# A two-layer megakernel: the plan of layer 0 with eight single PSUM banks

## Chip, cores and metric

One core of a Trainium2 chip runs the whole kernel in one launch. The metric is device time in microseconds. TensorE (PE) multiplies, VectorE (DVE) and ScalarE (ACT) read its results out of PSUM, GpSimd (POOL) works on SBUF alone, and SyncE (SP) issues the loads. PSUM has eight banks of 128 x 512 float32; TensorE writes a product into a bank, and another engine must read it before the bank can be written again.

## What is computed

Two layers over 2 sequences of 1024 tokens with 256 channels. The change touches only layer 0:

```python
# layer 0, attention: 16 query heads of 16 channels, 8 key/value heads
xn = layernorm(x)
q, k, v = xn @ W_Q.T, xn @ W_K.T, xn @ W_V.T
q, k = rope(q), rope(k)
scores = einsum('bsdkg,btdk->bkgst', q, k) / sqrt(256)
ctx = softmax(scores) @ v
s = ctx @ W_O.T
# layer 0, feed-forward: weights are a 16-entry table looked up by index
gate, up = xn @ lut[gate_idx].T, xn @ lut[up_idx].T
y = (silu(gate) * up) @ lut[down_idx].T
x = x + s * silu(y)
```

So the feed-forward does not need the attention, only its weights and xn; the two meet at the end. Layer 1 is a gated recurrence over 128-token chunks and a mixture of eight experts with a shared one; its code is the same in both kernels.

## The kernel before

**Blocks.** Attention runs in sixteen blocks (g, h): g counts batch and group of four heads, h the half of 512 queries. In a block the four heads lie in four groups of 32 rows of the TensorE array (`SLOT`), so matmuls of different heads, which have different rows, can run side by side. A block has four kinds of work:

- *maxima* (`largest`, L570 to L600): for each of 4 query chunks, 2 halves of the keys and 2 pairs of heads, TensorE makes the products mx of two heads (L582, two matmuls a head), and VectorE takes the largest of each row from both in one reduction (L598). 16 products and 16 reductions a block.
- *shift* (L602): from these maxima VectorE makes the negative shift, TensorE transposes it (mTp, L635), ScalarE copies it (mT, L642).
- *scores* (`weigh`, L644 to L668): for each of 8 key chunks and 2 pairs of heads, TensorE makes the transposed scores sc of two heads (L654, three matmuls a head: two of q and k, one that adds the shift), and ScalarE takes the exponential of each (L666). 16 products and 32 exponentials a block.
- *gather* (`gather`, L670): for each key chunk TensorE adds the four heads' exponentials times v into cx (L679, eight instructions in the trace). After the eighth, ScalarE copies cx, TensorE transposes it (ctp, L701) and VectorE divides (L708, L709).

**Other steps of layer 0.** `chunks` normalises, projects and rotates the tokens (qkv L439, transposes L411, L524); `project_out` makes s (so, L742); `decode` (L759) turns the indices into weights in nine pieces: for each of 16 table entries a comparison ("pick", L768) on GpSimd or, for the pieces of `DVE_PIECES`, on VectorE, and an addition on GpSimd (L785); `feed` (L795) is the feed-forward in four blocks of 512 tokens (gate and up L813, down L861), which needs all nine pieces. Its first two blocks compute silu by Tanh, which ScalarE has loaded together with Exp, the last two by Silu, which needs another table.

**The plan.** None of these steps is placed by hand. Each is an entry of the class `Plan`: an engine, a cost in us, what it reads and writes, and a due number `when`. `write_order` (L190) goes through a model of time: of all steps whose inputs are done and whose buffers are free it takes the one that can start first, and among those the one with the smallest `when`; it emits the step and moves the engine's clock on by the cost. The order in which steps are emitted is the order in which each engine will run them. A row product (maxima or scores) looks for a second one with other rows (`_mates`, L158); if there is one, the two are emitted as a team, round by round, so that four matmuls stand next to each other. `TURN` and `SOLO` are surcharges on `when` for a change of kind of work and for a row product without a mate.

**Buffers.** Slots are taken from pools when a step is placed (`_take`, L168) and come free after their last reader. The eight PSUM banks stand in three pools: "bank" with three single ones (scores and all transposes and projections), "pair" with two of two neighbouring banks each (maxima), "sum" with one (cx). The plan does not write the waits: the layer below it adds a semaphore wait wherever an instruction touches what another engine's earlier instruction touched.

Layer 1 follows in another order, made by the tile layer's own scheduler.

Of the kernel before, what the change touches and what calls it, by code (L numbers as in the profile page):

```python
# [11 lines left out]
F32 = mybir.dt.float32  # L12
# [8 lines left out]
P = 128  # L21
# [15 lines left out]
NQT = 4  # L37
# [58 lines left out]
class Plan:  # L96
# [71 lines left out]
    def _take(self, step):  # L168
        for t in step.slots:
            if t.slot is None:  # L170
                p = self.pools[t.pool]
                p["free"].sort()
                _, t.slot = p["free"].pop(0)
                p["held"][t.part] = p["held"].get(t.part, 0) + 1
                t.ap = p["pool"].tile(
                    list(t.shape), t.dtype, tag=f"{t.pool}{t.slot}", name=t.name, bufs=1
                )

    def _drop(self, step, end):
        for t in step.slots:  # L180
            t.left -= 1
            t.end = max(end, getattr(t, "end", 0.0))
            if t.left == 0:
                p = self.pools[t.pool]
                p["free"].append((t.end + 0.08, t.slot))
                p["held"][t.part] -= 1

    LAG = {"PE": 0.2, "ACT": 0.12, "DVE": 0.1, "POOL": 0.12, "SP": 0.0}

    def write_order(self, log=None):  # L190
# [4 lines left out]
        while left:  # L195
            best = None
            for e in self.ENGINES:
                if best and clock[e] > best[0]:
                    continue
                for s in ready[e]:  # L200
# [21 lines left out]
            if s.engine == "PE" and s.mode != mode:  # L222
                start += 0.1
            self._take(s)
            ready[s.engine].remove(s)
            if s.passes:
                for x in self._mates(s, ready["PE"], start + 0.05)[:1]:
                    team.append(x)
                    self._take(x)
                    ready["PE"].remove(x)  # L230
                rounds = max(len(x.passes) for x in team)
                for r in range(rounds):
                    for x in team:
                        if r < len(x.passes):
                            for _, emit in x.passes[r]:
                                emit()
                clock["PE"] = start + rounds * self.ROW
                ends = [start + len(x.passes) * self.ROW for x in team]
            else:
# [7 lines left out]
            for x, end in zip(team, ends):  # L247
                left -= 1
                self._drop(x, end)
                for y in x.next:  # L250
# [8 lines left out]
def first_layer(nc, tc, xs, xnT, s_sb, ident, epst, x_v, wqkv_d, rope_d, lut_d, idx_d, wo_d, sel_d):  # L259

    psum = bass.MemoryType.PSUM
    with ExitStack() as st:
        att = st.enter_context(tc.tile_pool(name="att", bufs=1))
        slots = st.enter_context(tc.tile_pool(name="slots", bufs=1))
        ps1 = st.enter_context(tc.tile_pool(name="ps1", bufs=1, space=psum))
        st.enter_context(tc.manual_schedule())
        plan = Plan(
            tc,
            {
                "bank": (ps1, [P, 512], 3, {}),  # L270
                "pair": (ps1, [P, 2, 512], 2, {}),
                "sum": (ps1, [P, 512], 1, {}),
                "two": (slots, [P, 512], 26, {"e": 13, "f": 16}),
                "q": (slots, [P, 512], 10, {}),
# [9 lines left out]

        def bank(name):
            return Slot("bank", [P, 512], name)

# [65 lines left out]
        STAT = 4  # L353
        qhls, kTs, qTs, tops, mTs, cxs, sums, ctxs, es = {}, {}, {}, {}, {}, {}, {}, {}, {}

# [213 lines left out]

        def largest(g, h, c, half, pair, when):  # L570

# [3 lines left out]
            top = tops[g, h]  # L575
            ps = Slot("pair", [P, 2, 512], f"mx{g}_{h}_{c}_{half}_{pair}")
            qT, kT = qTs[g, h], kTs[b, T // 2]

            def product(k, x):
                i = 2 * pair + k  # L580
                at = slice(SLOT * i, SLOT * (i + 1))
                nc.tensor.matmul(  # L582
                    ps.ap[:, k, :],
                    qT.ap[at, ts(c, P)],
# [9 lines left out]
            need = (qT, (kT, 2 * half), (kT, 2 * half + 1)) if half else (qT, (kT, 0), (kT, 1))  # L594
            add(PE, 0.43, None, need, (ps,), when, "rows", passes)

            def reduce():
                nc.vector.tensor_reduce(top.ap[:, c, 2 * pair : 2 * pair + 2, half], ps.ap, AX.X, ALU.max)  # L598

            add(DVE, 1.22, reduce, (ps,), ((top, c, half, pair),), when)  # L600

# [41 lines left out]

        def weigh(g, h, c, pair, when):  # L644
            b, T = divmod(g, NQT)
            qT, kT, mT = qTs[g, h], kTs[b, T // 2], mTs[g, h]
            pss = [bank(f"sc{g}_{h}_{c}_{2 * pair + k}") for k in range(2)]

# [9 lines left out]
            ]  # L658
            add(PE, 0.65, None, (qT, (kT, c // 2), mT, "sel"), pss, when, "rows", passes)
            for k in range(2):  # L660
                i = 2 * pair + k
                e = two(f"e{g}_{h}_{c}_{i}", part="e")
                es[g, h, c, i] = e

                def soft(k=k, e=e):
                    nc.scalar.activation(e.ap, pss[k].ap, AF.Exp, scale=1.0 / math.sqrt(E))  # L666

                add(ACT, 0.5, soft, (pss[k],), (e,), when + URGENT)  # L668

        def gather(g, h, c, when):  # L670
            b, T = divmod(g, NQT)
            if c == 0:
                cxs[g, h] = Slot("sum", [P, 512], f"cx{g}_{h}")
            cx = cxs[g, h]
# [84 lines left out]
        def decode(piece, when):  # L759
            at = slice(piece * LSTEP, (piece + 1) * LSTEP)  # L760
            codes = two(f"idx{piece}", I32)
            idx = lambda: codes.ap[:, 0:LSTEP]
            add(SP, 3.2, lambda: nc.sync.dma_start(idx(), idx_d[:, at]), (), (codes,), when - 4)
            for j in range(LUT):
                pick = two(f"pick{piece}_{j}") if j else None

# [11 lines left out]
                if piece in DVE_PIECES:  # L778
                    add(DVE, 0.63, choose, (codes, "lut"), (pick or ("w", piece),), w)
                else:  # L780
                    add(POOL, 1.2, choose, (codes, "lut"), (pick or ("w", piece),), w)
                if j:
# [127 lines left out]

        HALF = 8
        chunks(0, lambda c: -60 + 3 * c, True)
        order = [(g, h) for g in range(B * NQT) for h in range(2)]

        def maxima(k):
            g, h = order[k]
            w = HALF * (k - 1) - 4
            turn_q(g, h, w - 2 if k else -51)
            n = 0
            for half in range(2):  # L920
                for c in range(BC):
                    for pair in range(2):
                        largest(g, h, c, half, pair, w + n / 2 if k else -48 + n / 2 + 8 * half)
                        n += 1
            shift(g, h, w + HALF)

        def sums_of(k):
            g, h = order[k]
            w = HALF * k
            for c in range(CPB):  # L930
                for pair in (1, 0):
                    weigh(g, h, c, pair, w + c + (0.5 if pair == 0 else 0.0))
            for c in range(CPB):
                gather(g, h, c, w + c + 2)

        for piece in range(WLUT // LSTEP):
            decode(piece, DECODE_AT[piece])
        for k in range(len(order)):
            maxima(k)
            if k == 1:  # L940
                chunks(1, lambda c: 30 + 2.5 * c, False)
            sums_of(k)
            g, h = order[k]
            if g == NQT - 1:
                for c in range(h * BC, h * BC + BC, 2):
                    project_out(0, c, HALF * k + 14 + c)
            if g == 2 * NQT - 1:
                for c in range(h * BC, h * BC + BC, 2):
                    project_out(1, c, HALF * k + 14 + c)
        for n in range(NBLK):  # L950
# [571 lines left out]
```

## Time and profile before

| what | value |
|---|---|
| median of two runs | 1560.97 us (1558.97 to 1562.96) |
| profiled execution | 1572.11 us, of which the span from first to last instruction is 1570.3 |
| TensorE busy | 1384.5 us, 88% |
| VectorE, ScalarE, GpSimd busy | 743.7, 554.5, 478.0 us |
| mean granted TensorE clock | 0.925 |
| reductions of the maxima, L598 | 256, 304.4 us, 1219 ns each |
| exponentials, L666 | 512, 278.7 us, 595 ns each |
| gathers' matmuls, L679 | 1024, 145.6 us |
| comparisons of the decode on VectorE | 64, 792 ns each |
| table loads of ScalarE before L666, L830 and L875 | 33, 1283 ns each |

The page cuts the span into 40 slices of 39 us and gives each engine's busy share of a slice in tenths. A group's line gives the source line, engine, operation, tile, count, busy time, the mean of one, then the idle time of the engine just before these instructions and what ended it. In a timeline each row is a start, a duration and an instruction, with idle time before it in brackets. Matmuls are pipelined and each is recorded with its latency, so a busy TensorE is not one at its peak. The first matmul of layer 1 starts at 781.68 us.

### The profile page before, as it was taken

The numbers are of one execution on the slowest core, as the hardware profiler recorded it, in microseconds if no ns is written. First come the engines' busy times: TensorE is split into PE (matmuls) and PEld (weight loads), VectorE is DVE, ScalarE is ACT, GpSimd is POOL, SyncE is SP. The second block draws the span as 40 slices with busy tenths as digits, with TensorE's granted clock in tenths as the row PEclk, the third lists the DMA queues.
The fourth block names the chain that finished last, engine by engine and source line by source line (L and its number), as shares of the span: only waits on it lengthen the run. The fifth ranks groups of instructions, "written<-read, shape, count | busy, mean of one in ns | idle before, by whom it ended". The sixth has DMA issues, their size and how long they took to land. (4 is left out here: it accounts for less than half of the span.)

```text
span 1570.3 us, 18022 instructions
## 1 busy us (share of the span) xinstructions
PE 1384.5 (88%) x7272; PEld 730.6 (47%) x7272; DVE 743.7 (47%) x1055; ACT 554.5 (35%) x958; POOL 478.0 (30%) x401
## 2 busy tenths in 40 slices
PE   5899998999999998999686787877777999999998
PEld 2444443444444443434364354544555354453636
DVE  6878887786556444410254265533556312212120
ACT  5256555565544456666412311123211111101010
POOL 7999999896000000000201122210322000010101
PEclk9679998999999999999968889889899999999999
DMA  4000000000000000000220000000000100000000
GB/s 136 1 1 2 1 1 1 1 1 1 1 1 1 1 1 1 1 1 1 75 89 0 0 1 1 0 0 0 1 1 1 47 7 7 0 14 0 14 1 14
DMA packets 8019, 16.80 MB, mean 11 GB/s; under 512 B 1144, under 2 KB 6904, under 8 KB 7424
## 3 DMA queue, kind: packets, MB, share of 16 engines
q1 hardware_dynamic: 7760, 15.58, 2.8%
q8 instruction: 57, 0.93, 0.2%
q14 instruction: 26, 0.21, 0.0%
q10 hardware_dynamic: 144, 0.07, 0.0%
q0 software_dynamic: 32, 0.00, 0.0%
HBM read 13.55 MB, written 2.10 MB: 10 GB/s over the span
## 5 line engine op out<-in xcount | busy, mean ns | idle before, releaser
L598 DVE TENSOR_REDUCE top<-mx 128x2 f32<-128x1024 f32 x256 | 304.4, 1219 | 115.9 <-PE mx L582 98.7
L666 ACT ACTIVATE e<-sc 128x512 f32<-128x512 f32 x512 | 278.7, 595 | 201.4 <-PE sc L654 177.1
L654 PE MATMUL sc<-qT,kT 32*128 32x512 f32 x1024 | 223.7, 464 | 38.1 <-ACT e L666 36.4
L582 PE MATMUL mx<-kT,qT 32*128 32x512 f32 x1024 | 191.4, 461 | 4.9 <-DVE top L598 4.7
L654 PEld LDWEIGHTS sc<-qT,kT 32*128 32x128 f32 x1024 | 95.2, 191 | 209.2 <-issue 108.3
L1250 POOL TENSOR_TENSOR k<-d,kT 128x896 f32<-128x896 f32 x32 | 67.3, 2105 | 342.2 <-ACT d L1246 342.2
L785 POOL TENSOR_TENSOR wlut<-wlut,pick 128x480 f32<-128x480 f32 x135 | 164.6, 1226 | 8.4
L768 POOL TENSOR_SCALAR pick<-idx,lut 128x480 f32<-128x480 int32 x75 | 143.9, 1918 | 11.0 <-PE cx L679 5.3
L679 PE MATMUL cx<-e,v 128*32 128x512 f32 x1024 | 145.6, 629 | 0.8 <-ACT e L666 0.7
L654 PE MATMUL sc<-mT,sel 32*128 32x512 f32 x512 | 126.8, 406 | 0.0
L1400 POOL TENSOR_TENSOR g<-s_sb,g 128x256 f32<-128x256 f32 x16 | 11.6, 722 | 335.7 <-ACT g L1399 335.7
L1238 PE MATMUL dec<-cst,z 128*128 128x512 f32 x128 | 74.8, 704 | 41.9 <-DVE z L1215 31.5
L582 PEld LDWEIGHTS mx<-kT,qT 32*128 32x128 f32 x1024 | 91.6, 200 | 42.5 <-DVE top L598 18.7
L1367 PE MATMUL gu<-xnT,wg 128*128 128x512 f32 (+1 forms) x224 | 110.2, 614 | 1.1 <-issue 1.1
L1375 ACT ACTIVATE sg<-gu 128x512 f32<-128x512 f32 (+1 forms) x56 | 33.4, 597 | 213.5 <-PE gu L1367 213.5
L1367 PE MATMUL gu<-xnT,wu 128*128 128x512 f32 (+1 forms) x224 | 105.6, 593 | 0.0
L1385 DVE TENSOR_TENSOR sg<-sg,share 128x512 f32<-128x512 f32 x44 | 30.2, 687 | 144.5 <-PE share L1378 142.2
L1391 PE MATMUL d<-wd,h 128*128 128x256 f32 x448 | 97.4, 379 | 0.0
L1258 DVE TENSOR_TENSOR d<-d,rT 128x1024 f32<-128x1024 f32 x32 | 52.7, 1647 | 87.0 <-POOL end L1257 86.7
L1284 PE MATMUL lev<-d,k 64*128 64x128 f32 x896 | 76.8, 334 | 17.6 <-DVE d L1258 16.0
L1391 PEld LDWEIGHTS d<-wd,h 128*128 128x128 f32 x448 | 85.1, 190 | 13.5 <-issue 2.0
L1246 ACT ACTIVATE d<-dec 128x1024 f32<-128x1024 f32 x32 | 32.7, 1023 | 165.9 <-PE dec L1238 165.9
(181 smaller groups left out, 1740.8 us busy)
## 6 DMA issues: line engine op xcount, KB each, us to landing
idx<-in_idx SPq DMA_DIRECT2D x9, 240.0 KB, 4.8
out_x<-o SPq DMA_DIRECT2D x16, 128.0 KB, 1.7
wd<-in_wd SPq DMA_DIRECT2D x1, 1792.0 KB, 7.4
wg<-in_wg SPq DMA_DIRECT2D x1, 1760.0 KB
wu<-in_wu SPq DMA_DIRECT2D x1, 1760.0 KB, 12.9
xs<-in_x SPq DMA_DIRECT2D x3, 512.0 KB, 8.0
w<-in_w SPq DMA_DIRECT2D x1, 1536.0 KB, 8.4
cst<-in_cst SPq DMA_DIRECT2D x1, 576.0 KB, 5.4
```

What stands on the lines that cost most here:

```text
L582: nc.tensor.matmul(ps.ap[:, k, :], qT.ap[at, ts(c, P)], kT.ap[at, x, ts(half, 512)], start=(x == 0), stop=(x == 1),)
L598: nc.vector.tensor_reduce(top.ap[:, c, 2 * pair : 2 * pair + 2, half], ps.ap, AX.X, ALU.max)
L654: nc.tensor.matmul(pss[k].ap, lhsT, rhs, start=(x == 0), stop=(x == 2))
L666: nc.scalar.activation(e.ap, pss[k].ap, AF.Exp, scale=1.0 / math.sqrt(E))
L679: nc.tensor.matmul(cx.ap[SLOT * i : SLOT * (i + 1), :], vps[b][:, c, 4 * (T // 2) + i, :], ee[i].ap, start=(c == 0), stop=(c == CPB - 1),)
L768: eng.tensor_scalar(pick.ap[:, 0:LSTEP] if j else wlut[:, at], idx(), float(j), lut[:, j : j + 1], ALU.is_equal, ALU.mult,)
L785: nc.gpsimd.tensor_tensor(wlut[:, at], wlut[:, at], pick.ap[:, 0:LSTEP], ALU.add)
L1238: nc.tensor.matmul(ps[:, h, :], spl[:, k4, ts(m, P)], levels[:, ts(h, 512)], start=True, stop=True,)
L1250: nc.gpsimd.tensor_tensor(k, d[:, 0:NLEV, :], kT1[:, m : m + 1, tok].to_broadcast([P, NLEV, P]), ALU.mult,)
L1284: nc.tensor.matmul(psv[:, par, l2, m, :], lhsT, rhs, start=True, stop=True)
L1367: nc.tensor.matmul(ps[:sz, which, :], w[:, kc, lo : lo + sz], xnT[:, kc, ts(n, 512)], start=(kc == 0), stop=(kc == KC - 1),)
L1391: nc.tensor.matmul(po[:, 0:E], hT[:sz, f, ts(k, P)], wd1[:sz, f, :], start=(f == 0), stop=(f == NF1 - 1),)
```

## The change

Five things, all in layer 0 and its plan:

1. **PSUM.** The pools "bank", "pair" and "sum" become one pool of eight single banks, all views of one tile `banks` of 128 x 8 x 512. At most one is cx, four are maxima, four scores, three anything else ("aux"). A pair of maxima takes any two free banks, lower number first, and its reduction reads both through one access pattern with a step.
2. **Pairing.** `Plan` charges a lone row product in all cases, lets a product wait up to 0.2 us of plan time for its mate, and uses other costs and lags.
3. **Order.** Maxima run a fixed 24 products ahead of the scores, one maxima product due with each score product, with complementary pairs of heads. Batch 1's projections get other due numbers. Exponentials lose their surcharge of 500.
4. **Decode.** Pieces 6, 7 and 8 instead of 5 to 8 go to VectorE; all decode steps get due numbers from 1000 on, the index loads too, so that they come after anything else that could start.
5. **SBUF slots.** The 26 slots of the pool "two" are shared out otherwise: up to 12 for general use instead of 16, 3 for picks and 2 for indices.

In the built order of the changed kernel each engine runs the same work as before apart from the decode piece and 29 table loads less; matmuls of layer 0 are the same in number.

```diff
-DVE_PIECES = (5, 6, 7, 8)
+DVE_PIECES = (6, 7, 8)
-DECODE_AT = tuple(8 * k + (20 if k in DVE_PIECES else 0) for k in range(9))
+DECODE_AT = tuple(1000 + 8 * k for k in range(9))
+GATHER = 2
-    ROW = 0.214
+    ROW = 0.226
+    WAIT = 0.2
-        if engine in ("ACT", "DVE") and any(isinstance(v, Slot) and v.pool == "bank" for v in reads):
+        if engine in ("ACT", "DVE") and any(isinstance(v, Slot) and v.part == "aux" for v in reads):
             when -= URGENT
...
+        new = [t for t in step.slots if t.slot is None]
+        for name in {t.pool for t in new}:
+            p = self.pools[name]
+            p["free"].sort()
+            mine = [t for t in new if t.pool == name]
+            got = sorted(k for _, k in p["free"][: len(mine)])
+            del p["free"][: len(mine)]
+            for t, t.slot in zip(mine, got):
                 p["held"][t.part] = p["held"].get(t.part, 0) + 1
+                if name == "bank":
+                    t.ap = p["pool"][:, t.slot, :]
...
-    LAG = {"PE": 0.2, "ACT": 0.12, "DVE": 0.1, "POOL": 0.12, "SP": 0.0}
+    LAG = {"PE": 0.22, "ACT": 0.17, "DVE": 0.15, "POOL": 0.15, "SP": 0.0}
...
-                        if s.passes and at <= clock[e] and not self._mates(s, ready[e], at):
+                        if s.passes and not self._mates(s, ready[e], at + self.WAIT):
                             late += self.SOLO
...
-                for x in self._mates(s, ready["PE"], start + 0.05)[:1]:
+                for x in self._mates(s, ready["PE"], start + self.WAIT)[:1]:
+                    start = max(start, x.ready, self._room(x))
...
+        banks = ps1.tile([P, 8, 512], F32, name="banks")
-                "bank": (ps1, [P, 512], 3, {}),
-                "pair": (ps1, [P, 2, 512], 2, {}),
-                "sum": (ps1, [P, 512], 1, {}),
-                "two": (slots, [P, 512], 26, {"e": 13, "f": 16}),
+                "bank": (banks, [P, 512], 8, {"sum": 1, "mx": 4, "sc": 4, "aux": 3}),
+                "two": (slots, [P, 512], 26, {"e": 13, "f": 12, "d": 3, "i": 2}),
...
-            ps = Slot("pair", [P, 2, 512], f"mx{g}_{h}_{c}_{half}_{pair}")
+            pss = [bank(f"mx{g}_{h}_{c}_{half}_{2 * pair + k}", "mx") for k in range(2)]
...
             def reduce():
-                nc.vector.tensor_reduce(top.ap[:, c, 2 * pair : 2 * pair + 2, half], ps.ap, AX.X, ALU.max)
-            add(DVE, 1.22, reduce, (ps,), ((top, c, half, pair),), when)
+                lo, hi = pss[0].slot, pss[1].slot
+                i = 2 * pair
+                nc.vector.tensor_reduce(
+                    top.ap[:, c, i : i + 2, half], banks[:, lo : hi + 1 : hi - lo, :], AX.X, ALU.max
+                )
...
+        for i in range(LEAD):
+            w = -48 + i / 2 + (8 if i >= 8 else 0)
+            products(w, maximum(i, w))
+            if i == 15:
+                shift(*order[0], w)
+        for s in range(16 * len(order)):
+            k, j = divmod(s, 16)
+            g, h = order[k]
+            w = s / 2
+            c, pair = j // 2, 1 - j % 2
+            if s == 100:
+                chunks(1, lambda c: 54 + 2 * c, False)
+            products(w, weigh(g, h, c, pair))
+            i = s + LEAD
+            if i < 16 * len(order):
+                products(w, maximum(i, w))
+            if i % 16 == 15 and i < 16 * len(order):
+                shift(*order[i // 16], w)
+            if pair == 0:
+                gather(g, h, c, w + GATHER)
```

`products` adds one TensorE step for the parts it is given, here always one, and then its readers; `maximum` returns the i-th maxima product.

More of the change, by code (lines that the diff above doesn't have):

```diff
@@ L168, in _take @@
     def _take(self, step):
[L169 to L173, printed above, removed]
-                p["held"][t.part] = p["held"].get(t.part, 0) + 1
-                t.ap = p["pool"].tile(
-                    list(t.shape), t.dtype, tag=f"{t.pool}{t.slot}", name=t.name, bufs=1
-                )
+        new = [t for t in step.slots if t.slot is None]
[6 more added lines that the diff above has]
+            for t, t.slot in zip(mine, got):
+                p["held"][t.part] = p["held"].get(t.part, 0) + 1
+                if name == "bank":
+                    t.ap = p["pool"][:, t.slot, :]
+                else:
+                    t.ap = p["pool"].tile(
+                        list(t.shape), t.dtype, tag=f"{name}{t.slot}", name=t.name, bufs=1
+                    )
     def _drop(self, step, end):
@@ L184, in _drop @@
                 p = self.pools[t.pool]
-                p["free"].append((t.end + 0.08, t.slot))
+                p["free"].append((t.end, t.slot))
                 p["held"][t.part] -= 1
-    LAG = {"PE": 0.2, "ACT": 0.12, "DVE": 0.1, "POOL": 0.12, "SP": 0.0}
+    LAG = {"PE": 0.22, "ACT": 0.17, "DVE": 0.15, "POOL": 0.15, "SP": 0.0}
     def write_order(self, log=None):
@@ L223, in write_order @@
                 start += 0.1
+            turn = 0.1 if s.passes and s.mode != mode else 0.0
             self._take(s)
@@ L236, in write_order @@
                                 emit()
-                clock["PE"] = start + rounds * self.ROW
-                ends = [start + len(x.passes) * self.ROW for x in team]
+                clock["PE"] = start + rounds * self.ROW + turn
+                ends = [start + len(x.passes) * self.ROW + turn for x in team]
             else:
@@ L248, in write_order @@
                 left -= 1
-                self._drop(x, end)
+                self._drop(x, end + self.LAG[x.engine])
                 for y in x.next:
@@ L283, in first_layer, with bank @@
         add = plan.add
-        def bank(name):
-            return Slot("bank", [P, 512], name)
+        def bank(name, part="aux"):
+            return Slot("bank", [P, 512], name, F32, part)
         def two(name, dtype=F32, part="f"):
@@ L353, in first_layer @@
         STAT = 4
-        qhls, kTs, qTs, tops, mTs, cxs, sums, ctxs, es = {}, {}, {}, {}, {}, {}, {}, {}, {}
+        qhls, kTs, qTs, tops, mTs, cxs, es, es_all = {}, {}, {}, {}, {}, {}, {}, {}
         def chunks(b, when, first):
@@ L568, in turn_q, with largest @@
             add(ACT, 0.5, lambda: nc.scalar.copy(qT.ap, ps.ap), (ps,), (qT,), when)
-        def largest(g, h, c, half, pair, when):
+        def largest(g, h, c, half, pair):
             b, T = divmod(g, NQT)
@@ L582, in product @@
                 nc.tensor.matmul(
-                    ps.ap[:, k, :],
+                    pss[k].ap,
                     qT.ap[at, ts(c, P)],
@@ L594, in largest @@
             need = (qT, (kT, 2 * half), (kT, 2 * half + 1)) if half else (qT, (kT, 0), (kT, 1))
-            add(PE, 0.43, None, need, (ps,), when, "rows", passes)
             def reduce():
-                nc.vector.tensor_reduce(top.ap[:, c, 2 * pair : 2 * pair + 2, half], ps.ap, AX.X, ALU.max)
-            add(DVE, 1.22, reduce, (ps,), ((top, c, half, pair),), when)
+                lo, hi = pss[0].slot, pss[1].slot
+                i = 2 * pair
+                nc.vector.tensor_reduce(
+                    top.ap[:, c, i : i + 2, half], banks[:, lo : hi + 1 : hi - lo, :], AX.X, ALU.max
+                )
+            return (need, pss, passes), lambda w: add(
+                DVE, 1.14, reduce, pss, ((top, c, half, pair),), w
+            )
         def shift(g, h, when):
@@ L642, in shift, with weigh @@
             add(ACT, 0.5, lambda: nc.scalar.copy(mT.ap, ps.ap), (ps,), (mT,), when)
-        def weigh(g, h, c, pair, when):
+        def weigh(g, h, c, pair):
             b, T = divmod(g, NQT)
             qT, kT, mT = qTs[g, h], kTs[b, T // 2], mTs[g, h]
-            pss = [bank(f"sc{g}_{h}_{c}_{2 * pair + k}") for k in range(2)]
+            pss = [bank(f"sc{g}_{h}_{c}_{2 * pair + k}", "sc") for k in range(2)]
             def product(k, x):
@@ L658, in weigh, with soft, act, rest @@
             ]
-            add(PE, 0.65, None, (qT, (kT, c // 2), mT, "sel"), pss, when, "rows", passes)
             for k in range(2):
[L661 to L665, printed above, removed]
+                es[g, h, c, 2 * pair + k] = two(f"e{g}_{h}_{c}_{2 * pair + k}", part="e")
+            def soft(k):
+                e = es_all[g, h, c, 2 * pair + k]
+                def act():
                     nc.scalar.activation(e.ap, pss[k].ap, AF.Exp, scale=1.0 / math.sqrt(E))
-                add(ACT, 0.5, soft, (pss[k],), (e,), when + URGENT)
+                return e, act
+            es_all.update({(g, h, c, 2 * pair + k): es[g, h, c, 2 * pair + k] for k in range(2)})
+            def rest(w):
+                for k in range(2):
+                    e, act = soft(k)
+                    add(ACT, 0.49, act, (pss[k],), (e,), w)
+            return ((qT, (kT, c // 2), mT, "sel"), pss, passes), rest
+        def products(when, *parts):
+            need, pss, passes = [], [], []
+            for (n, p, q), _ in parts:
+                need += n
+                pss += p
+                for r, x in enumerate(q):
+                    if r == len(passes):
+                        passes.append([])
+                    passes[r] += x
+            add(PE, 0.0, None, need, pss, when, "rows", passes)
+            for _, rest in parts:
+                rest(when)
         def gather(g, h, c, when):
@@ L672, in gather @@
             if c == 0:
-                cxs[g, h] = Slot("sum", [P, 512], f"cx{g}_{h}")
+                cxs[g, h] = bank(f"cx{g}_{h}", "sum")
             cx = cxs[g, h]
@@ L760, in decode @@
             at = slice(piece * LSTEP, (piece + 1) * LSTEP)
-            codes = two(f"idx{piece}", I32)
+            codes = two(f"idx{piece}", I32, "i")
             idx = lambda: codes.ap[:, 0:LSTEP]
-            add(SP, 3.2, lambda: nc.sync.dma_start(idx(), idx_d[:, at]), (), (codes,), when - 4)
+            add(SP, 3.2, lambda: nc.sync.dma_start(idx(), idx_d[:, at]), (), (codes,), when)
             for j in range(LUT):
-                pick = two(f"pick{piece}_{j}") if j else None
+                pick = two(f"pick{piece}_{j}", part="d") if j else None
                 def choose(j=j, pick=pick, eng=nc.vector if piece in DVE_PIECES else nc.gpsimd):
@@ L778, in decode @@
                 if piece in DVE_PIECES:
-                    add(DVE, 0.63, choose, (codes, "lut"), (pick or ("w", piece),), w)
+                    add(DVE, 0.75, choose, (codes, "lut"), (pick or ("w", piece),), w)
                 else:
-                    add(POOL, 1.2, choose, (codes, "lut"), (pick or ("w", piece),), w)
+                    add(POOL, 1.92, choose, (codes, "lut"), (pick or ("w", piece),), w)
                 if j:
@@ L911, in first_layer @@
         HALF = 8
+        LEAD = 24
         chunks(0, lambda c: -60 + 3 * c, True)
         order = [(g, h) for g in range(B * NQT) for h in range(2)]
[L915 to L934, printed above, removed]
         for piece in range(WLUT // LSTEP):
             decode(piece, DECODE_AT[piece])
[L938 to L942, printed above, removed]
-            g, h = order[k]
-            if g == NQT - 1:
+        def maximum(i, when):
+            k, j = divmod(i, 16)
+            g, h = order[k]
+            if j == 0:
+                turn_q(g, h, when - 2)
+            half, c, pair = j // 8, j // 2 % 4, j % 2
+            return largest(g, h, c, half, pair)
@@ new lines, in first_layer @@
+        for i in range(LEAD):
[18 more added lines that the diff above has]
+                gather(g, h, c, w + GATHER)
+            if j == 15 and g % NQT == NQT - 1:
@@ L945, in first_layer @@
                 for c in range(h * BC, h * BC + BC, 2):
[L946 to L949, printed above, removed]
+                    project_out(g // NQT, c, w + 6 + c)
         for n in range(NBLK):
```

## Prediction

> **What bounds the kernel now.** I read the page's slices first, then the windows, then the timeline of one stretch, then the groups.
>
> ```profile
> PE   5899998999999998999686787877777999999998
> ...
> DVE  6878887786556444410254265533556312212120
> ACT  5256555565544456666412311123211111101010
> POOL 7999999896000000000201122210322000010101
> ```
>
> A slice is 39 us. Layer 0 fills the first twenty; layer 1, which the change does not touch, the rest. TensorE looks full all through layer 0, and GpSimd is full until about slice 10, where the decode of the feed-forward weights ends.
>
> ```profile
> core 0: us, PE busy (x) PEld busy (x) DVE busy (x) ACT busy (x) POOL busy (x), PEclk, DMA share, GB/s
> 122.50:344.70 222.20, 203.73 (x1474) 94.22 (x1472) 178.73 (x206) 123.87 (x241) 208.28 (x154) 0.93 0.00 1
> 344.70:768.70 424.00, 399.30 (x2415) 188.33 (x2413) 181.64 (x224) 234.19 (x386) 45.80 (x35) 0.96 0.00 1
> 850.00:900.00 50.00, 37.52 (x158) 21.73 (x158) 21.46 (x33) 13.77 (x16) 5.12 (x6) 0.86 0.00 0
> ```
>
> Each row is a stretch, its length and the busy times; the last row lies in layer 1. The first row runs from the end of attention block 1 (its ctp transposes, at 122.51) to that of block 8 (344.71): 222.2 / 7 = 31.7 us a block. The second is blocks 9 to 16 with the feed-forward between them, 53 us a block.
>
> ```profile
> 331.84 0.50 PE L654 MATMUL sc<-qT,kT 32*128 32x512 f32 x2
> 331.85 0.49 PE L582 MATMUL mx<-kT,qT 32*128 32x512 f32 x2
> ...
> 332.41 0.39 PE L654 MATMUL sc<-mT,sel 32*128 32x512 f32 x2
> 332.63 2.35 DVE L598 TENSOR_REDUCE top<-mx 128x2 f32<-128x1024 f32 x2 [0.47 <-PE mx L582]
> ...
> 332.84 1.09 ACT L666 ACTIVATE e<-sc 128x512 f32<-128x512 f32 x2 [0.96 <-PE sc L654]
> ...
> 333.49 0.72 PE L654 MATMUL sc<-qT,kT 32*128 32x512 f32 x3 [0.22 <-ACT e L666]
> ...
> 334.37 1.06 PE L679 MATMUL cx<-e,v 128*32 128x512 f32 x8
> ```
>
> Four matmuls start within 0.01 us of each other, so a round costs the same with two as with four. Rounds follow each other by 0.23 us, the first of a team by 0.33; a team of three rounds takes PE 0.9 us, one of two 0.57, a gather 1.0. From the start of a team to its reader: 0.8 to 1.0 for scores, 0.73 to 0.8 for maxima. A reduction takes 1.22 and the next follows after 1.14; an exponential 0.6 and the next after 0.5. A waiter restarts 0.07 to 0.11 after what releases it. By these a block is some 25 us of PE work (57 rounds, 8 gathers, 3 transposes), so 6 of its 31.7 are waits hidden in "busy": mostly for one of three score banks.
>
> ```profile
> L582 PE MATMUL mx<-kT,qT 32*128 32x512 f32 x1024 | 191.4, 461 | 4.9 <-DVE top L598 4.7
> ...
> L785 POOL TENSOR_TENSOR wlut<-wlut,pick 128x480 f32<-128x480 f32 x135 | 164.6, 1226 | 8.4
> L768 POOL TENSOR_SCALAR pick<-idx,lut 128x480 f32<-128x480 int32 x75 | 143.9, 1918 | 11.0 <-PE cx L679 5.3
> ```
>
> The groups: TensorE hardly ever waits for a reduction now, and the decode has GpSimd to itself.
>
> **Part by part**, in the time of the profiled execution (span 1570.3, whole 1572.1, against a median of 1561.0; I carry the difference over to the median). Counts of the changed kernel are from its built order of instructions and waits, which holds no time.
>
> *Fewer rounds.* 849 against 920: 71 x 0.23 = 16 us of PE. This is part of p below. The pairing changes its kind: 167 rounds of four are scores with scores and 97 maxima with maxima (11 and 18 before), 167 mixed (331 before). 418 rounds still hold only two matmuls.
>
> *Decode.* DVE drops one piece: 16 x 0.79 = 12.7 us less there, GpSimd 16 x 1.92 = 30.7 more, so its part ends near 382 + 31 = 413 instead of 382, where the first feed matmul stands now. But the new order puts the first feed behind block 12, and that is at about 590 by the sum below: zero, with 180 us of cover; without that cover it would be the 31. The nine index loads are moved behind everything else in SP's queue, where nothing waits that layer 0 needs (2 go out at once, 7 as their slots come free): zero, as each lands in 4.8 us and is held a whole piece ahead. The 48 picks left on DVE (38 us) move from blocks 1 to 8 to blocks 8 to 13, now queued between reductions: half on the path, 19, ends 0 and 38.
>
> *Table loads.* 29 ACT_TABLE_LOADs of 1.28 us go, because the exact Silu blocks come after the last exponential: 37 us of ACT, which waits for PE 109 us in that stretch anyway. I book zero; up to 20 saved lies in my range.
>
> *Eight single banks.* Two reads of layer 0 now hang together that didn't: the reduction reads two banks of one tile with a step, and the built order treats everything from the lower to the higher as read. 208 of 256 pairs are not neighbours. So 159 times TensorE waits for a reduction of banks that it does not write, 140 times ScalarE does, and the reductions wait 127 times for a matmul and 111 for an exponential in a bank between theirs. Behind a waiting TensorE instruction stands all of its queue, gathers and feed included; behind a waiting reduction the later reductions, hence shift and mT; behind an exponential the gather. No row of before shows such a wait, so I worked one block of the new order (the fourth, with fewer of these waits than most) through by the durations above. Along the chain that ends last lie eleven of its sixteen reductions, 13.4 us; eight row teams from release to result, 0.73 to 1.1 each, 7.2; five exponentials with restart, 3.5; four runs of PE work without a break (three gathers, ten teams, the qT transposes), 11.0; and ctp with its share, then shift with mTp and mT, 4.1. Sum p = 39.2 us. Bounds: 25 (PE work alone, no false wait on the path), 42 (block three, which has more of them, worked the same way). I take 39.
>
> [...]
>
> *Sum for the end of layer 0's PE work.* Block 1 ends at 122.5 as now (7 less for the picks, up to 17 more for its 30 waits for reductions). Blocks 2 to 14: 13p. Batch 1's projections and transposes (12 x 0.98 + 28 x 0.14), which the 31.7 contained: 15. Picks 19, out-projection 4. Blocks 15 and 16 have hardly a reduction: 16 teams x 0.9 + 8 gathers = 22.4, take 24 each, 48. Feed within blocks 13 to 16 (54 gate/up instructions of 0.98, 48 down of 0.5; 77 us): half of the 39 in blocks 13 and 14 and all in the two PE-bound ones, 57. Feed behind block 16, where PE had 6.5: 34 x 0.98 + 48 x 0.5 + out-projection and last copy 7 = 64. Together 329.5 + 13p = 836.5 at p = 39, against 775.2, where the last out-projection matmul ends now: +61. Break-even is p = 34.3; 2% (31 us) lies at 31.9 and 36.7.
>
> *Clock.* Rows: 0.97 to 1.0 where PE is full, 0.86 at 37.5 busy of 50. At 0.9, 13 blocks x 25 us of PE work x 0.08 = 26 more, if all lies on the path; I leave it in the range. [...]
>
> **The rivals.** (1) *The waits are over before they bind:* p is PE's 25 plus two for DVE and ACT: 329.5 + 351 = 680, which is 95 less, 1466, faster. For it: eight banks in one pool where scores now have three, DVE and ACT at 20 us a block each. Against: the worked chain, in which eleven reductions stand one after another. It decides below p = 32. (2) *Partly hidden*, p near 34: the waits fall beside exponentials that were late anyway, and the time is 1557, no change. For it: 6 us a block are waits already, and more banks remove them. (3) *GpSimd becomes the bound:* its picks take slots that a gather must free, so a slow block delays the decode; it decides only if the decode ends after block 12, and would add at most the 31 us moved there, 1653; against it stand 350 us of decode (96 x 1.92 + 135 x 1.23) in 590. That the change does not do what it says is excluded: the order has three pieces on DVE and the single banks.
>
> **How the numbers follow.** Forecast 0.70, of which 0.62 slower and 0.08 within 2%; rival 1 0.12, all faster; rival 2 0.15 (0.01 faster, 0.12 same, 0.02 slower); rival 3 0.03 (0.02 slower, 0.01 same). So faster 0.13, same 0.21, slower 0.66; 2% is about what a measurement of this kernel can tell. Time 1561 + 61 = 1622. Range: low end p = 36 with picks and feed hidden (-39 - 19 - 20 + 61 = -17) and the start's 7 less, 1537; high end p = 42 (+39), start, picks and feed on the path to the half of their 56 (+28), 1689. Below it lies rival 1 (0.12), above it some 0.05.
>
> **What would show it.** Right: blocks of 37 to 42 us between ctp transposes; idle of PE before L591's and L668's matmuls put down to DVE's reductions, which hardly occurs now (4.7 us); feed matmuls first near 590; clock below 0.93 in slices 4 to 14. Wrong: blocks under 34, ACT and DVE above 70% busy, layer 0 over before 740.

## The result, and the profile after

The changed kernel takes 1720.63 us (median of 2 runs, 1717.62 to 1723.64) against 1560.97 before: 1.1023 times as long, interval 1.0920 to 1.1126. It is slower, as forecast, but by 160 us instead of 61, and lies above the range.

The busy shares of the changed kernel's span, in 40 slices of 43 us:

```profile
PE   5678778878888888988998876777777899999998
...
DVE  5743445554355446544113443653446521212030
...
POOL 7845555667365423000011012230032201010101
PEclk9655778887587768997998788898988999999999
```

TensorE, full all through layer 0 before, now has mostly 7 or 8 tenths there, and VectorE and GpSimd went down with it: no engine is busy throughout, and all of them wait. The granted clock is well below full speed in most slices up to the sixteenth, and the decode on GpSimd ends about there instead of near slice 10.

Three stretches of the changed kernel, with length, busy times and clock: from 50 us to the end of block 1, blocks 2 to 12, and from there to about the end of layer 0:

```profile
core 0: us, PE busy (x) PEld busy (x) DVE busy (x) ACT busy (x) POOL busy (x), PEclk, DMA share, GB/s
50.00:149.30 99.30, 72.89 (x363) 34.22 (x364) 49.16 (x53) 27.36 (x53) 59.77 (x43) 0.55 0.01 3
149.30:674.20 524.90, 425.33 (x2694) 190.43 (x2693) 258.29 (x297) 220.92 (x424) 277.43 (x197) 0.76 0.01 4
674.20:925.00 250.80, 230.91 (x1201) 112.65 (x1199) 90.45 (x132) 94.81 (x175) 17.55 (x14) 0.93 0.00 1
```

The second row is the heart of the matter: 524.9 / 11 = 47.7 us a block, TensorE idle for 100 of 525 us, and its clock at 0.76. Before, the same eleven blocks took 457.8 us at a clock of 0.94, with part of the feed-forward among them. The kernel before has one stretch like this too, at its start:

```profile
50.00:100.00 50.00, 44.76 (x201) 21.63 (x204) 36.62 (x45) 15.66 (x34) 47.24 (x37) 0.60 0.00 0
```

A piece of the changed kernel's timeline in block 4 (start, length, engine and work, idle before it and what ended that):

```profile
250.81 2.35 DVE L608 TENSOR_REDUCE top<-banks 128x2 f32<-128x1024 f32 x2 [2.53 <-PE banks L591]
...
253.22 0.73 PE L668 MATMUL banks<-qT,kT 32*128 32x512 f32 x8 [1.52 <-DVE top L608]
...
254.26 1.57 ACT L680 ACTIVATE e<-banks 128x512 f32<-128x512 f32 x3 [2.87 <-PE banks L668]
254.91 0.50 PEld L591 LDWEIGHTS banks<-kT,qT 32*128 32x128 f32 x4 [0.70 <-ACT e L680]
...
256.24 1.23 DVE L608 TENSOR_REDUCE top<-banks 128x2 f32<-128x1024 f32 x1 [3.08 <-PE banks L591]
```

VectorE, TensorE, ScalarE, TensorE, VectorE: each starts just after the piece of work that released it. VectorE and ScalarE were idle for 2.5 to 3.1 us before, TensorE's matmuls for 1.5 and its weight loads (PEld) for 0.7. The score matmuls at 253.22 stand behind two reductions of maxima, with which they share no data. In the built order the first of them writes bank 2 and waits for the second of these reductions, which reads banks 1 and 4.

The groups of the changed kernel that answer to those of before (busy, mean ns of one, idle before and its main releaser; L591 makes the maxima, L668 the scores):

```profile
L608 DVE TENSOR_REDUCE top<-banks 128x2 f32<-128x1024 f32 x256 | 309.3, 1222 | 333.6 <-PE banks L591 131.4
...
L591 PE MATMUL banks<-kT,qT 32*128 32x512 f32 x1024 | 214.8, 548 | 53.2 <-DVE top L608 44.7
L668 PE MATMUL banks<-qT,kT 32*128 32x512 f32 x1024 | 198.5, 534 | 57.1 <-DVE top L608 51.9
...
L805 POOL TENSOR_SCALAR pick<-idx,lut 128x480 f32<-128x480 int32 x90 | 171.3, 1904 | 125.9 <-PE banks L716 102.4
L822 POOL TENSOR_TENSOR wlut<-wlut,pick 128x480 f32<-128x480 f32 x135 | 163.5, 1215 | 132.4 <-DVE pick L805 109.7
```

TensorE's maxima waited 4.7 us for reductions before and wait 44.7 now; its scores, whose main wait before was 36.4 us for exponentials, wait 51.9 for reductions. The strided reduction itself costs what the dense one did: 1222 ns against 1219. And a maxima matmul takes 548 ns instead of 461, for the same work.

### The profile page after: what moved, and what is told of

It is laid out like the page before. It is cut to its first block, busy times and chain, and to the rows that moved or that the text cites. A ratio compares the mean times of both kernels' runs of the same rounds, so it can differ in the third digit from the quotient of the medians.

```text
span 1721.7 us, 18082 instructions
## 1 busy us (share of the span) xinstructions
PE 1447.1 (84%) x7272; PEld 754.3 (44%) x7272; DVE 716.2 (42%) x1039; ACT 511.9 (30%) x929; POOL 504.0 (29%) x417
## 5 line engine op out<-in xcount | busy, mean ns | idle before, releaser
L608 DVE TENSOR_REDUCE top<-banks 128x2 f32<-128x1024 f32 x256 | 309.3, 1222 | 333.6 <-PE banks L591 131.4
L680 ACT ACTIVATE e<-banks 128x512 f32<-128x512 f32 x512 | 276.8, 601 | 368.5 <-PE banks L668 182.9
L591 PE MATMUL banks<-kT,qT 32*128 32x512 f32 x1024 | 214.8, 548 | 53.2 <-DVE top L608 44.7
L668 PE MATMUL banks<-qT,kT 32*128 32x512 f32 x1024 | 198.5, 534 | 57.1 <-DVE top L608 51.9
L716 PE MATMUL banks<-e,v 128*32 128x512 f32 x1024 | 177.4, 775 | 18.7 <-DVE top L608 17.4
L668 PEld LDWEIGHTS banks<-qT,kT 32*128 32x128 f32 x1024 | 89.2, 229 | 181.7 <-DVE top L608 99.2
L591 PEld LDWEIGHTS banks<-kT,qT 32*128 32x128 f32 x1024 | 98.7, 238 | 151.6 <-DVE top L608 82.2
L668 PE MATMUL banks<-mT,sel 32*128 32x512 f32 x512 | 109.2, 469 | 0.0
L850 PE MATMUL banks<-xnT,wlut 128*128 128x512 f32 (+1 forms) x176 | 82.3, 617 | 3.6 <-DVE top L608 3.6
L1334 DVE COPY_PREDICATED w<-msk,lev 128x512 f32<-128x512 int32 x112 | 81.1, 724 | 7.0 <-DVE w L1334 0.5
```

The source lines that it names most:

```text
L591: nc.tensor.matmul(pss[k].ap, qT.ap[at, ts(c, P)], kT.ap[at, x, ts(half, 512)], start=(x == 0), stop=(x == 1),)
L608: nc.vector.tensor_reduce(top.ap[:, c, i : i + 2, half], banks[:, lo : hi + 1 : hi - lo, :], AX.X, ALU.max)
L668: nc.tensor.matmul(pss[k].ap, lhsT, rhs, start=(x == 0), stop=(x == 2))
L716: nc.tensor.matmul(cx.ap[SLOT * i : SLOT * (i + 1), :], vps[b][:, c, 4 * (T // 2) + i, :], ee[i].ap, start=(c == 0), stop=(c == CPB - 1),)
L850: nc.tensor.matmul(ps.ap[:m, :], wgu[:, kc, lo : lo + m], xnT[:, kc, ts(n, 512)], start=(kc == 0), stop=(kc == KC - 1),)
L1334: nc.vector.copy_predicated(w, msk[:, lev, :].unsqueeze(1).unsqueeze(1).to_broadcast([P, 2, 2, P]), psv[:, :, l2],)
```

## The experiments

One theory against two rivals: **false waits** (the reduction's read over two banks of one tile bars every bank between them, and these waits set the chain), **rival A** (the order by passes and its new costs are at fault) and **rival B** (the moved decode is). All times but those of e1_adjacent and e2_timed are one run each; the kernel before gave 1560 to 1575 us beside them.

**Split the reduction, keep everything else** (e2_split, timed as e2_timed). Order and banks are those of the changed kernel on TensorE, ScalarE and GpSimd; VectorE has each reduction in two halves at its place.

```diff
-                nc.vector.tensor_reduce(
-                    top.ap[:, c, i : i + 2, half], banks[:, lo : hi + 1 : hi - lo, :], AX.X, ALU.max
-                )
+                for k in range(2):
+                    i = 2 * pair + k
+                    nc.vector.tensor_reduce(
+                        top.ap[:, c, i : i + 1, half], pss[k].ap, AX.X, ALU.max
+                    )
```

> The changed kernel with the same plan, the same order on every engine and the same banks; only the one reduction over two banks is written as two, one for each bank, so that it reads only its own. VectorE gets 256 instructions more; if each half takes just over half of the 1.22 us, this is 10 to 30 us of VectorE over the layer, beside TensorE. Theory of the false waits: the order stands and the stalls go, blocks 28 to 36 us, 1460 to 1570 us. Rivals A and B: the order and the decode are unchanged, so 1700 us or more. This is the sharpest of the four, since nothing but the span of the read differs.

> The changed kernel with split reductions again, now timed in rounds against the kernel before: 1430 to 1450 us, a ratio of 0.91 to 0.93, by every theory; the look before gave 1438.

Measured: 1438.4 us, and timed 1443.31 (1438.14 to 1445.52), 0.9209 of the kernel before, interval 0.9153 to 0.9264. This is lower than the theory's range (1460 to 1570). Blocks 2 to 12 of the split kernel, and the groups of its reductions and of its maxima:

```profile
105.90:425.20 319.30, 308.84 (x2695) 148.31 (x2693) 274.49 (x474) 214.33 (x426) 282.90 (x200) 1.00 0.02 6
```

```profile
L608 DVE TENSOR_REDUCE top<-banks 128x1 f32<-128x512 f32 x512 | 318.2, 681 | 54.2 <-PE banks L591 51.7
...
L591 PE MATMUL banks<-kT,qT 32*128 32x512 f32 x1024 | 171.9, 457 | 5.7 <-ACT e L680 3.6
```

29.0 us a block instead of 47.7, with the same matmuls (2695 records against 2694) in the same order. TensorE's idle time falls from 99.6 to 10.5 us, its busy time from 425.3 to 308.8, and the clock comes back to 1.00. Splitting costs VectorE 9 us of busy time (318 against 309) and nothing that shows. Since nothing but the form of the read differs, rivals A and B are out. (Two short reads could also help by freeing each bank sooner; the next experiment keeps the one long read.) Who waits tells it too. The changed kernel's longest waits in blocks 2 to 12, then those of the split one (us in total, times, longest):

```profile
ACT e L680 <- DVE top L608: 139.9, 71, 4.6
ACT e L680 <- PE banks L668: 114.3, 73, 4.4
DVE top L608 <- PE banks L591: 99.2, 52, 4.8
```

```profile
ACT e L680 <- PE banks L668: 87.9, 96, 2.5
DVE top L608 <- PE banks L591: 35.4, 50, 2.1
```

An exponential needs nothing that a reduction makes. In the split kernel, and in the kernel before, no exponential's idle time is put down to a reduction at all.

**Give a pair neighbouring banks** (e1_adjacent). The plan picks two free banks k and k+1 for maxima; the reduction stays one.

```diff
+    def _near(self, p):
+        free = {k: at for at, k in p["free"]}
+        pairs = [(max(free[k], free[k + 1]), k) for k in free if k + 1 in free]
+        return min(pairs) if pairs else None
...
-            got = sorted(k for _, k in p["free"][: len(mine)])
+            if mine[0].part == "mx":
+                k = self._near(p)[1]
+                got = [k, k + 1]
...
```

> The changed kernel, but the plan gives the two banks of a maxima pair as neighbours (k and k+1), so that the reduction on VectorE reads no bank that is not its own. Theory (false waits of the reduction on the banks between its two set the chain, and the stalls they leave make the TensorE clock fall): blocks 2 to 12 of layer 0, measured from one division's transposes to the next, take 27 to 34 us instead of 47.7, the clock in 150 to 675 us comes back from 0.75 to about 0.9, and the time is 1450 to 1545 us. Rival A (the order by passes, the lower cost 1.14 and the new due numbers are at fault, not the banks): blocks above 43 us and 1650 to 1750 us. Rival B (the decode on VectorE and GpSimd lies on the path): no different from rival A here, 1680 us or more.

Measured: 1445.59 us (1439.86 to 1451.10), 0.9237 of before, interval 0.9178 to 0.9296; the time is just below the theory's range, the blocks of 29.1 us lie in it, and the clock of 1.00 is above the 0.9 named. Its blocks 2 to 12:

```profile
105.50:425.90 320.40, 311.62 (x2694) 150.83 (x2694) 264.21 (x296) 215.67 (x426) 283.54 (x200) 1.00 0.02 6
```

With no bank between the two the read may span them, and it is still one read: the gain doesn't come from shorter reads, and the theory is confirmed a second way. (The split kernel and this one can't be told apart.)

**Old pools in the changed kernel** (e3_old_pools: "bank" 3, "pair" 2, "sum" 1 again, pairing and decode of the change kept).

```diff
-                "bank": (banks, [P, 512], 8, {"sum": 1, "mx": 4, "sc": 4, "aux": 3}),
+                "bank": (ps1, [P, 512], 3, {}),
+                "pair": (ps1, [P, 2, 512], 2, {}),
+                "sum": (ps1, [P, 512], 1, {}),
...
```

> The changed kernel with the three PSUM pools of before (three single banks, two pairs, one sum); the order by passes, the new numbers and the new decode stay. Theory of the false waits: they are gone, and with them the gain in banks, so near the kernel before: blocks 31 to 36 us and 1530 to 1600 us. Rivals A and B: 1650 us or more.

Measured: 1515.35 us, blocks 33.8 us. The blocks lie in the theory's range, the time is a little below it: without its banks the change is a gain over before.

**The banks alone in the kernel before** (e4_before_banks: the one tile of eight banks and the strided reduction, nothing else of the change; the plan orders its steps anew), and **the same with split reductions** (f4_before_split).

> The kernel before with the change's banks alone: all eight from one tile, and the reduction reading two of them with a step; order without pairing, costs and decode as before. Theory of the false waits: most of the loss comes with this part alone, 1640 to 1760 us, blocks above 41 us and a TensorE clock in the layer's first half below that of before. Rivals A and B: 1540 to 1590 us, as before.

> The kernel before with the change's eight banks and the reductions split in two, but without pairing by passes, without the new numbers, and with the decode of before. Against the changed kernel with split reductions and the old decode (1467 us) it leaves out the pairing and the new numbers. If the banks alone carry the gain: 1450 to 1485 us. If the pairing by passes is worth what the prediction's step on rounds said (16 us) or more: 1483 to 1520 us. If false waits were not the cause of the 1766 us of the same kernel with the read over two banks: 1700 us or more.

Measured: 1766.42 us (blocks 50.0, clock 0.77), just above the theory's range, and 1484.38 us (blocks 32.7, clock 0.97), where the two ranges for the banks and the pairing meet. The banks alone, strided, bring more than the whole loss: some 205 us, of which the rest of the change gave about 46 back (1766 to 1721). Read singly, they bring 77 of the gain (1561 to 1484). Blocks 2 to 12 of e4, and waits of exponentials for reductions over its whole span:

```profile
166.70:716.70 550.00, 439.40 (x2740) 197.55 (x2738) 271.46 (x313) 224.67 (x430) 234.07 (x172) 0.77 0.00 1
```

```profile
ACT e L675 <- DVE top L605: 181.3, 90, 5.7
```

**The old decode** (f3_split_old_decode: split reductions, four pieces on VectorE and the early due numbers).

```diff
-DVE_PIECES = (6, 7, 8)
+DVE_PIECES = (5, 6, 7, 8)
-DECODE_AT = tuple(1000 + 8 * k for k in range(9))
+DECODE_AT = tuple(8 * k + (20 if k in DVE_PIECES else 0) for k in range(9))
```

> The changed kernel with split reductions (1438 us) and the decode of before: four pieces of nine on VectorE, early due numbers. If the move of the decode was worth something by itself, this is slower than 1438 by VectorE's or GpSimd's share: VectorE is busy for 0.8 to 0.97 of 300 to 450 us there, so 5 to 25 us slower; if the decode is covered on both sides, within 10 us of 1438.

Measured: 1467.51 us, 22 to 29 slower than the runs of the split kernel, at or above the top of the range for a move that matters; its blocks 5 to 9 take 186.1 us together against 157.3. So the moved decode is worth some 25 us where the false waits are gone. The step from f4 to f3, 17 us, is then all else of the change: pairing, order, costs and SBUF slots together. It lies between two single runs, and runs of the kernel before differ by up to 15 us among themselves, so its size is not well known.

**Does more work bring the clock back?** Five kernels keep the false waits, and four of them add useless matmuls to TensorE. e5_double issues the first matmul of each maxima product twice. f1_seven only takes a bank from the plan; the other three write fillers to that bank: f2_filler one of 32 rows behind the pair of matmuls that ends each row product, f5_filler3 three, f6_filler_full one of 128 rows. The edit of f2_filler, of which the same lines behind the scores are left out here:

```diff
-                "bank": (banks, [P, 512], 8, {"sum": 1, "mx": 4, "sc": 4, "aux": 3}),
+                "bank": (banks, [P, 512], 7, {"sum": 1, "mx": 4, "sc": 4, "aux": 3}),
...
+                if x == 1 and k == 1:
+                    nc.tensor.matmul(
+                        banks[:, 7, :],
+                        qT.ap[0:SLOT, ts(c, P)],
+                        kT.ap[0:SLOT, x, ts(half, 512)],
+                        start=True,
+                        stop=True,
+                    )
...
```

> The changed kernel with the same order on VectorE, ScalarE and GpSimd and the same banks; on TensorE every first matmul of a maxima row product is issued twice, 512 matmuls more (32 in a block of layer 0, of 0.23 us each at the full clock: 7.4 us a block). They write the bank of the product, so they stand behind its wait and lengthen the chain; the outputs stay as they are. Theory A (TensorE drops to half its clock in a window of 3.41 us that follows a full window in which it was busy for under about 0.55 of the time, and comes back only after one in which it was busy for over about 0.85): more work in the windows keeps the clock up, so it is above the 0.75 of the changed kernel in 150 to 675 us, 0.80 or more, and the blocks grow by less than the work put in: 44 to 52 us. Theory B (the clock falls for another cause, time or power, and more work doesn't raise it): clock 0.75 or less and blocks of 47.7 plus 7.4 / 0.75 = 57.5 us, 1870 us.

> The changed kernel with seven banks in the plan instead of eight, the eighth unused: the kernel that the next is compared with. False waits remain; there are fewer banks between the two of a pair, and fewer to go round. 1680 to 1780 us by every theory, blocks of 45 to 51 us, clock 0.72 to 0.80.

> The kernel with seven banks, with the same order, plus one useless matmul behind each of the 512 row products' pairs of layer 0 (256 maxima, 256 scores), written to the eighth bank, which nobody reads: it waits for nothing but the pair before it, so it runs where TensorE would stand and wait for the next bank. No result uses it. Theory A (the clock follows TensorE's activity in windows of 3.41 us): fewer half windows, clock in 150 to 675 us above 0.85, and blocks shorter than those of the kernel with seven banks in spite of 7.4 us more work: by 0 to 6 us, 1600 to 1720 us. Theory B (another cause): the clock as there, blocks 3 to 10 us longer, 1730 us or more.

> The kernel with seven banks and three useless matmuls behind each pair of row products instead of one (1536 of them in layer 0, 22 us a block at the full clock). The blocks can't be short any more, so the clock tells: by the rule of busy windows (theory A; one filler took the busy share only from 0.81 to 0.86 and the clock from 0.755 to 0.780, since a half window must be busy for over about 0.85 to bring the clock back) the busy share in blocks 2 to 12 is now above 0.93, the clock above 0.90, and blocks 50 to 58 us, 1760 to 1890 us. By another cause of the clock (theory B) it stays at 0.75 to 0.79 and the blocks grow to 60 us or more, 1900 us.

> As the kernel with seven banks and one useless matmul behind each pair of row products (1785 us, blocks 51.0, clock 0.780, TensorE busy 0.858 of blocks 2 to 12), the same number at the same places, but each over all 128 rows of the array instead of 32. Three fillers of 32 rows had made TensorE busy for 0.949 of the time and the clock had fallen to 0.692, so the busy share in the records is not what the clock follows. Theory A (the clock follows how much of the array is at work): clock above 0.85 in blocks 2 to 12, and blocks shorter than 51.0 although a change between 32-row and 128-row matmuls can cost something: 41 to 50 us, 1600 to 1770 us. Theory B (more work on TensorE only lengthens the chain and does not raise the clock): clock 0.70 to 0.78 and blocks of 52 to 65 us, 1800 us or more.

Measured, in blocks 2 to 12:

| kernel | time, us | block, us | TensorE busy | clock |
|---|---|---|---|---|
| changed | 1720.6 | 47.7 | 0.81 | 0.76 |
| e5_double | 1742.4 | 48.9 | 0.83 | 0.79 |
| f1_seven | 1749.5 | 49.3 | 0.81 | 0.75 |
| f2_filler | 1784.9 | 51.0 | 0.86 | 0.78 |
| f5_filler3 | 2071.7 | 70.1 | 0.95 | 0.69 |
| f6_filler_full | 2045.3 | 67.3 | 0.93 | 0.75 |

f1 came as expected. e5 lies near theory A (its block in the range, its clock of 0.79 just short of 0.80) and far from theory B's 1870 us; the three with fillers miss theory A in clock and in time, and f5's clock lies below theory B's too. In e5 and f2, 7.4 us of added work lengthens a block by only 1.1 and 1.6 us, and the clock rises by 0.03. Of these 81 us in eleven blocks TensorE's idle time took up 8 and 22; where the rest went was not followed up. With three fillers TensorE is busy for 0.95 of the time and its clock falls further. f6's blocks grow by 18 us over f1's, about its 32 fillers of some 0.6 us (609 ns each behind the maxima, 597 behind the scores). So work put in raised the clock by 0.03 at most, and the busy share of a whole stretch does not tell it. Of what was tried, only the kernels without false waits brought it back.

## Why the prediction was wrong in size

- *Eight single banks: right in kind.* The direction, the false waits and their place were as worked out, and no other part of the change is to blame (e2, e1, e4).
- *The price p of a block: the step that failed.* It was taken as 39, with 42 as its upper bound. Blocks 2 to 12 took 524.9 us; without the 38 us that the sum booked apart for batch 1's projections, the picks and the out-projection that is p = 44.3. Two things lie in it, and how they share the miss stays open:
  - *The clock, booked at zero.* The chain was priced with durations of rows at a clock of 0.93 to 1.0. The prediction left 26 us for a fall to 0.9 "in the range", but the range as added up has no term for it. In blocks 2 to 12 the clock was 0.76, and in the 99 us before them 0.55. The same matmuls were busy for 425.3 us against 308.8 in the split kernel: 116.5 of the 205.6 us between the two, the other 89 being idle time. How much of the 116.5 lay on the chain isn't known, since no kernel kept the waits and the clock: p at full clock lies between some 34 (all of it) and 44 (none), with 39 in the middle. The prediction's reading of rows, "0.97 to 1.0 where PE is full", passed over the row of before shown above, where TensorE is busy for 0.90 of 50 us at a clock of 0.60.
  - *The block it was worked on.* Block 4 was taken for all, though it has, in the prediction's words, "fewer of these waits than most". Worked at 39.2, it took 41.5; block 3, worked at 42, took 48.7. The six blocks without batch 1's projections and out-projection (2, 3, 4, 10, 11, 12) took 46.0 on average, the last three with picks among their reductions.
- *Clock and gaps.* The sum has no term for a lower clock, and no run shows that a chain like this one keeps the full clock. In blocks 2 to 12 the longest gap between TensorE's matmuls is 1.91 us, and the clock was 0.76 all the same, against 1.00 in the split kernel.
- *Sum.* Block 1 ended at 149.3, not at 122.5 as before: +27, for which I had "up to 17" (in the split kernel it ended at 106). Block 12 was to end near 590 and ended at 674: another 58 from blocks 2 to 12. From there to the last matmul of layer 0 (930.9) it was 257 instead of 247: +10. Together (26.8 + 57.9 + 9.7) the end came 94 us later than 836.5. Layer 1 gave back 4, and the profiled run of before stood 8 us further above its median than that of the changed kernel: 98 of the 99 us between 1622 and 1720.6.
- *Fewer rounds.* The 16 us booked can't be told apart: the 17 us from f4 to f3 holds the order, costs and SBUF slots too, so that the two agree proves nothing. *Decode:* the prediction had no gain in it and 19 us of cost for the picks; without the false waits the move is worth about 25 us. What it does with them wasn't tried.
- *Table loads* were not timed apart. e4 and f4 have 25 in all, as the changed kernel has, against 54 before, so they went with the banks and their new plan, and not with the pairing.
- *Rivals.* The first, waits that don't bind, was priced at 1466; it is false for this kernel, but the split one is that case, and took 1443. The split kernel uses the same banks, and none of its exponentials' idle time is put down to a reduction: the wait came from how the program tracks a strided read, not from the banks. Of the third: GpSimd's decode did slow with the blocks (picks waited 102 us for gathers, 5 before) and ended at 697 us instead of 382. The first feed matmul came at 700, not 590, in block 13, so the 180 us of cover had shrunk to 3; but none of TensorE's idle time before the feed's gate and up matmuls is put down to the decode.
- *Signs.* TensorE's idle time put down to reductions, the clock under 0.93 in slices 4 to 14 and the feed behind block 12 came as named; blocks of 37 to 42 us did not.

## What to carry to other kernels

When buffers become slices of one tile, look in the built order for waits between instructions that share no buffer: a strided read over two slices can bar all between them, and here one read written as two was worth 16% of the time (1720.6 to 1443.3, the same order otherwise). Price a chain of waits on TensorE with durations at a lower clock as well as at the present one, since here the clock fell with the waits (0.76 in blocks 2 to 12, 1.00 in the split kernel), and price it on a block with as many waits as most. And take a change apart before it is dropped: here the banks (77 us), the decode (about 25) and, as far as single runs tell, the pairing with the rest (17) were gains, hidden under one access pattern.

## What the runs showed of the hardware

In the traces of before and of the changed kernel the clock was granted in windows of 3.41 us, full or half: of their 68 and 106 clock records, each at 1.00 or 0.50, all but the last of each trace are 3.41 us or a whole multiple of it long. Here are six such windows of the changed kernel:

```profile
200.08:203.49 3.41, 3.10 (x27) 1.33 (x27) 1.39 (x2) 1.09 (x2) 1.77 (x2) 1.00 0.00 0
203.49:206.90 3.41, 1.47 (x20) 0.88 (x16) 1.23 (x2) 1.55 (x3) 3.11 (x2) 1.00 0.00 0
206.90:210.32 3.42, 1.48 (x8) 0.70 (x12) 1.23 (x1) 0.85 (x3) 0.00 (x0) 0.50 0.01 2
210.32:213.73 3.41, 3.41 (x21) 1.34 (x15) 1.78 (x4) 0.86 (x2) 1.58 (x1) 0.50 0.00 0
213.73:217.14 3.41, 2.64 (x24) 1.65 (x21) 1.23 (x1) 2.63 (x6) 1.51 (x2) 1.00 0.00 0
217.14:220.56 3.42, 3.10 (x33) 0.92 (x29) 2.36 (x2) 1.59 (x4) 1.70 (x1) 1.00 0.00 0
```

The window after the one with TensorE busy for 1.47 of 3.41 us is at half clock; after one that is busy throughout, it is full again. Counted over both traces: of 66 full windows that were busy for under 0.55 of the time, 54 were followed by a half one, and of 567 that were busy for 0.80 or more, 2. Of 65 half windows that were busy for under 0.80, none was followed by a full one; of 126 with 0.90 or more, 80. So in blocks 2 to 12 of the changed kernel gaps of at most 1.91 us, added up within a window, went with half clock, and in these two traces no half window led back that was busy for under 0.86. But that does not tell all of it: of 98 half windows that were busy for 0.97 or more, 30 stayed half, and over blocks 2 to 12 TensorE was busy for 0.95 of the time with three fillers, at a clock of 0.69, and for 0.94 before, at a clock of 0.94. What the clock follows beyond this stays open.
